# Spreading the unpacking of 4-bit weights over three stages of a transformer block

## The chip, the cores and the metric

The kernel runs on one core of one Trainium2 chip. The metric is the device time of one execution in microseconds. A core has five engines that run side by side, each through its own instructions strictly in order: TensorE (PE in the profile; its weight loads are PEld), VectorE (DVE), ScalarE (ACT), GpSimd (POOL) and SyncE (SP, which here issues transfers only). Transfers (DMAs) are issued by SP, ACT or POOL and are carried by 16 DMA engines that all of them share.

## The reference

Two batches of 1024 tokens, width 1024, everything in 32-bit floats. A layer norm feeds two branches, and their product is added to the input:

```
xn = layernorm(x)                         # (2, 1024, 1024)
q, k = rope(xn @ wq), rope(xn @ wk)       # 32 heads of 32, 8 key/value heads
s  = softmax(causal(q k^T / sqrt(32))) v @ wo
w_gu, w_d = sc[g] * (nibble(qw) - (nibble(qz)[g] + 1))    # 4-bit weights, groups of 128 rows
gate, up = split(xn @ w_gu)               # 2 x 2752 columns
h  = silu(gate) * up
out = x + s * silu(h @ w_d)
```

The 4-bit weights come packed, eight to a 32-bit word along the rows.

## The kernel before

The stages run in this order: norm of batch 0; then for each batch the projection (q, k, v), the attention and the output projection (with wo); then the FFN of both batches. The norm of batch 1 is computed inside the output projection of batch 0.

**Unpacking (`unpack`, L234).** The packed weights are turned into 32-bit floats once, in units, and written to memory in the order in which the FFN loads them: 22 units for the gate and up weights (tensors ng), 12 for the down weights (nd). A unit (`unit`, L238) loads the words (qw, L242) and the zeros (zt, L244) on SP's queue; VectorE masks or shifts the words and adds the zeros (nib, L250 to L255), twice, for the even and the odd nibbles; ScalarE turns the bytes into floats (nf, L259), twice; GpSimd issues the stores (L267). It is a generator: it yields after each of these steps, five times in a unit, and whoever drives it calls `next`. All its buffers come from a pool of three. In batch 0 it makes the units 0 to 16 of gate and up, in batch 1 the other five and all of down, both in the output projection.

**Output projection (`project_out`, L872).** The result is made in 16 parts of 256 tokens by 256 columns, 16 matmuls each (ps_wo, L846). The first two parts are interleaved with the end of the attention (`first`), the other 14 follow here, in six PSUM buffers. At the beginning of each part `next(side)` is called three times, which advances the unpacking; after each part but the first, one tile of 128 tokens of the next batch's norm follows (`norm`, L299: load xt, statistics, std on ScalarE, xn on VectorE, eight transposes ps_ln on TensorE, two copies xnT on ScalarE). Even parts are copied out by VectorE and stored on GpSimd's queue, odd ones by ScalarE and stored on its own (`leave`, wo_r L858, sT L859). What the generator has left is called after the loop.

**Projection (`project`, L336).** k, then q, in blocks of 512 tokens by 128 columns, eight matmuls each (ps_qk, L354; three PSUM buffers). VectorE makes two products of a block (rot, L358 and L360), GpSimd two more operations (L361, L362), ScalarE rounds the result (rot_hi, L364), VectorE takes the rest (rot_lo, L366), and SP stores both halves (ks, qs). The finished keys and queries of the first head group are loaded again as stacks (room, L474 and L479), and TensorE multiplies them between the blocks of the later heads, to find each row's maximum (`rows`, `turns`; s, L514 and L520; VectorE reduces, mx L530). Beside that xn is split into two halves (x_hi L404, x_lo L406) and stored for the FFN (xs, L407 and L408). The argument `side` is advanced once after each block; in batch 0 it is a survey of the scales (`look`), in batch 1 it is empty.

**Attention (`attend`, L571).** Its order is written out by hand in steps of 128 keys. The score products for the maxima of later steps are spread over the steps by a planner; `due` forces those that a coming step needs. When a group is complete, `shifts` reduces the maxima on VectorE (mt, L554), and a step later `shift_rows` transposes them on TensorE (m_ps, L565) for use in the products of the step after that.

Outside the attention, a scheduler orders the instructions of each engine when the kernel is built, by what they depend on; `issue_after` puts an instruction behind a given one. The FFN (L1160) takes PSUM banks that the output projection used, and ScalarE and VectorE take turns at rescaling its accumulators (L930, L932).

Of the kernel before, what the change touches and what calls it, by code (L numbers as in the profile page):

```python
# [23 lines left out]
P = 128  # L24
# [12 lines left out]
def block_kernel(  # L37
# [193 lines left out]
        nc.vector.tensor_scalar(flag, ps, 1.0, None, ALU.min)  # L231
        yield

    def unpack(pool, b):  # L234

        def unit(r, qw_src, z_src, dst, w):  # L238
            qw = pool.tile([P, 2 * P], U32, name="qw")
            zt = pool.tile([P, 2 * P, 2], U16, name="zt")  # L240
            for c0, n, src in qw_src:
                nc.sync.dma_start(qw[:r, c0 : c0 + n], src)  # L242
            for c0, n, src in z_src:
                nc.sync.dma_start(zt[:r, c0 : c0 + n, :], src)  # L244
            nf = pool.tile([P, 4, 2, 2 * P], F32R, name="nf")
            nib = pool.tile([P, 2, 4 * P], U16, name="nib")
            halves = qw.bitcast(U16)
            for i in range(2):
                if i == 0:
                    nc.vector.tensor_scalar(nib[:r, i, : 2 * w], halves[:r, : 2 * w], 0x0F0F, None, ALU.bitwise_and)  # L250
                else:
                    nc.vector.tensor_scalar(
                        nib[:r, i, : 2 * w], halves[:r, : 2 * w], 4, 0x0F0F, ALU.logical_shift_right, ALU.bitwise_and
                    )
                nc.vector.tensor_tensor(  # L255
                    nib[:r, i, : 2 * w], nib[:r, i, : 2 * w], zt.rearrange("p n i -> p (n i)")[:r, : 2 * w], ALU.add
                )
                yield
                nc.scalar.activation(  # L259
                    nf[:r, :, i, :w],  # L260
                    nib[:r, i, :].bitcast(U8).rearrange("p (n b) -> p b n", b=4)[:, :, :w],
                    AF.Copy,
                    bias=-16.0,
                )
                yield
            for c0, n, to in dst:
                nc.gpsimd.dma_start(to, nf[:r].rearrange("p b i n -> p (b i) n")[:, :, c0 : c0 + n].bitcast(F32))  # L267
            yield
# [8 lines left out]
        for f in range(17) if b == 0 else range(17, NF):  # L277
            n = P if f < NF - 1 else FTAIL
            at = [(u * n, n, slice(u * INTER + f * P, u * INTER + f * P + n)) for u in range(2)]
            yield from unit(  # L280
                P,
                [(c0, n, qw_gu[:, cols]) for c0, n, cols in at],
                [(c0, n, zb_gu[:, cols]) for c0, n, cols in at],
                [(u * n, n, to) for u, to in enumerate(ng_rows(f, n))],
                2 * n,
            )
        for r0 in range(0, RD, P) if b == 1 else ():
            r1 = min(RD, r0 + P)
            for c0 in range(0, D, 2 * P):
                cols = slice(c0, c0 + 2 * P)  # L290
                yield from unit(
                    r1 - r0,
                    [(0, 2 * P, qw_d[r0:r1, cols])],
                    [(0, 2 * P, zb_d[r0:r1, cols])],
                    [(0, 2 * P, nd_dram.rearrange("(r s) n -> r s n", s=8)[r0:r1, :, cols])],
                    2 * P,
                )

    def norm(b, xnT, pool, psp, bufs):  # L299

        for t in range(NT):
            xt = pool.tile([P, D], F32, name="xt", bufs=bufs)
            nc.sync.dma_start(xt, x[b, t * P : (t + 1) * P, :])
            stats = pool.tile([P, 2, 6], F32, name="stats")
            for h in range(2):
                nc.vector.bn_stats(stats[:, h, :], xt[:, h * 512 : (h + 1) * 512])
            mv = pool.tile([P, 2], F32, name="mv")
            nc.vector.bn_aggr(mv, stats.rearrange("p h s -> p (h s)"))
            std = pool.tile([P, 1], F32, name="std")
# [4 lines left out]
            nc.vector.tensor_scalar(xn, xt, mv[:, 0:1], rstd, ALU.subtract, ALU.mult)  # L314
            for h in range(NS // 4):
                ps = psp.tile([P, 4, P], F32, name="ps_ln")
                for j in range(4):
                    nc.tensor.transpose(ps[:, j, :], xn[:, (4 * h + j) * P : (4 * h + j + 1) * P], ident)
                nc.scalar.copy(xnT[:, 4 * h : 4 * h + 4, t * P : (t + 1) * P], ps)
            yield  # L320

    def load_w(pool, w_dram, c, **kw):
        return load_w_at(pool, w_dram, c, **kw)[0]
# [12 lines left out]
    def project(b, xnT, w_k, qs, ks, v, side, head):  # L336


        with tc.tile_pool(name="qkv_w", bufs=3, reuse_waits="tile") as wp, tc.tile_pool(name="qkv", bufs=3, reuse_waits="tile") as pool, tc.tile_pool(
# [9 lines left out]
            def turned(w, dst, work=iter(()), blocks=range(NB)):  # L349
                for n in blocks:  # L350
                    tok = slice(n * TB, (n + 1) * TB)
                    ps = psp.tile([P, TB], F32, name="ps_qk")
                    for s in range(NS):
                        nc.tensor.matmul(ps, w[:, s, :], xnT[:, s, tok], start=(s == 0), stop=(s == NS - 1))  # L354
# [216 lines left out]
    def attend(head, v, oT, output):  # L571
# [5 lines left out]
        with ExitStack() as st:  # L577
# [165 lines left out]

# [16 lines left out]
            for i, (g, qb, kt) in enumerate(steps):  # L760
# [111 lines left out]
    def project_out(output, side, turns, xnT, xp):  # L872

        with ExitStack() as st:
# [4 lines left out]
            if xnT is not None:  # L879
                ln = st.enter_context(tc.tile_pool(name="ln", bufs=3, reuse_waits="tile"))  # L880
                ln_ps = st.enter_context(tc.tile_pool(name="ln_ps", bufs=2, space=PSUM, reuse_waits="tile"))
                following = norm(output.b + 1, xnT, ln, ln_ps, 3)
                w_k = load_kv(xp, wk)
            for i, part in enumerate(output.parts):
# [10 lines left out]
            for _ in following:  # L895
                pass
            return w_k

    def load_gu(ring, f, u):
# [509 lines left out]
    for b in range(B):  # L1409
# [5 lines left out]
        with tc.tile_pool(name="at_first", bufs=1, reuse_waits="tile") as fp, tc.tile_pool(  # L1415
# [5 lines left out]
            with tc.tile_pool(name="ps_s", bufs=1, space=PSUM, reuse_waits="tile") as ps_s:  # L1421
# [83 lines left out]
```

## Time and profile before

| what | us |
|---|---|
| median of three runs | 2325.3 (2325.21 to 2326.38) |
| profiled execution | 2326.46 |
| its span, first to last instruction | 2324.7 |
| TensorE busy | 2244.4 (97%) |
| VectorE / ScalarE / GpSimd busy | 1423.5 / 1132.7 / 799.1 |

The stages by their first matmul in the trace: projection of batch 0 at 26.6, its attention at 214, the rest of its output projection at 550.8; projection of batch 1 at 689.4, attention at 869, output projection at 1205.4; the FFN at 1304.2. "Busy" counts from an instruction's start to its end. Idle time is put down to what ended it, "<-" and the engine, operation and line. A wait on TensorE costs time; one on another engine costs only if TensorE comes to wait for it.

### The profile page before, as it was taken

To read this page: it belongs to the slowest core of one execution; us is meant where nothing else is said; L and a number is where in the kernel's file an instruction comes from. 1 tells how busy PE (TensorE), PEld (TensorE's weight loads), DVE (VectorE), ACT (ScalarE), POOL (GpSimd) and SP (SyncE) were. 2 spreads that over 40 slices of the span, in tenths; PEclk is the share of its full clock that TensorE was granted. 3 is DMA by queue.
4 is the path that set the end of the run, shared out by engine and by line. 5 is a ranking of instruction groups with operands and counts; after the bars stand their busy time and mean duration, and the time that the engine had idled before them with its cause. 6 is when DMAs were issued, how large, how long until landed. Compare 5 with 4: busy or idle time off the path is not lost.

```text
span 2324.7 us, 30824 instructions
## 1 busy us (share of the span) xinstructions
PE 2244.4 (97%) x11313; PEld 1549.1 (67%) x11313; DVE 1423.5 (61%) x2270; ACT 1132.7 (49%) x1819; POOL 799.1 (34%) x569
## 2 busy tenths in 40 slices
PE   7999999999699999999999899999999999999987
PEld 4456555557574465555558778888877888888765
DVE  6473777763422526777722367667877777767775
ACT  3013545453430015445533465555787655557775
POOL 1332677773313216777742100000235100001352
PEclk9999999999899999999999899999999999999999
DMA  6664131315974251231229632231746645323465
GB/s 197 215 226 120 46 92 46 80 31 172 298 268 154 91 142 49 49 89 37 73 80 324 213 82 60 77 82 55 281 148 216 179 137 139 101 59 114 153 202 149
DMA packets 262183, 309.50 MB, mean 133 GB/s; under 512 B 19147, under 2 KB 197707, under 8 KB 261880
## 3 DMA queue, kind: packets, MB, share of 16 engines
q1 hardware_dynamic: 245172, 260.62, 37.3%
q0 software_dynamic: 10752, 38.02, 5.1%
q10 hardware_dynamic: 6100, 8.82, 1.2%
q8 instruction: 91, 1.49, 0.3%
q14 instruction: 68, 0.56, 0.1%
HBM read 214.58 MB, written 97.03 MB: 134 GB/s over the span
## 4 chain that ended last, share of the span: by engine, by line
PE 68%; issue 11%; POOL 8%; DMA 5%; DVE 5%; ACT 2%; SPq 1%; POOLq 0%; ACTq 0%; DVEq 0%
PE acc L1160 27%; PE acc L1043 11%; PE s L520 6%; PE st L627 5%; PE o L674 5%; PE ps_wo L846 3%; PE l L692 3%; PE ps_v L374 2%; PE st L642 2%; POOL rot L361 2%; POOL rot L362 2%; PE ps_qk L354 2%; DMA qw<-in_L_ffn_qweight_gu 2%; POOL p L787 1%; DVE mx L530 1%
## 5 line engine op out<-in xcount | busy, mean ns | idle before, releaser
L1160 PE MATMUL acc<-x,w 128*128 128x512 f32 x2752 | 644.3, 395 | 9.2 <-ACT wo_r L858 6.2
L1160 PEld LDWEIGHTS acc<-x,w 128*128 128x128 f32 x2752 | 515.5, 189 | 129.6 <-DVE h L1133 7.5
L530 DVE TENSOR_REDUCE mx<-s 128x1 f32<-128x512 f32 (+3 forms) x672 | 384.2, 607 | 215.0 <-PE s L520 117.4
L932 DVE TENSOR_SCALAR acc<-acc,r_gu 128x1024 f32<-128x1024 f32 x301 | 389.0, 1293 | 178.2 <-PE acc L1160 177.6
L652 ACT ACTIVATE p<-st 128x512 f32<-128x512 f32 (+3 forms) x768 | 314.9, 496 | 312.1 <-PE st L642 312.0
L930 ACT ACTIVATE acc<-acc,r_gu 128x1024 f32<-128x1024 f32 x301 | 327.4, 1088 | 236.3 <-PE acc L1160 227.9
L1144 POOL TENSOR_TENSOR h_lo<-h,h_hi 128x512 fp32r<-128x512 f32 x78 | 100.4, 1289 | 803.6 <-PE acc L1043 588.7
L787 POOL TENSOR_TENSOR p<-p 128x2048 f32<-128x2048 f32 (+3 forms) x122 | 360.7, 2961 | 8.7 <-PE o L674 4.3
L932 DVE TENSOR_SCALAR acc<-acc,r_d 128x512 f32<-128x512 f32 x320 | 241.6, 758 | 67.7 <-PE acc L1043 65.0
L930 ACT ACTIVATE acc<-acc,r_d 128x512 f32<-128x512 f32 x320 | 210.9, 662 | 65.9 <-PE acc L1043 59.1
L354 PE MATMUL ps_qk<-xnT,w_qk 128*128 128x512 f32 x512 | 238.9, 604 | 0.0
L846 PE MATMUL ps_wo<-oT,w_o 128*128 128x256 f32 x1024 | 236.4, 387 | 0.0
L1043 PE MATMUL acc<-h_lo,w 128*128 128x512 f32 (+1 forms) x576 | 228.9, 397 | 2.9 <-POOL h_lo L1144 2.8
L1043 PE MATMUL acc<-h_hi,w 128*128 128x512 f32 (+1 forms) x576 | 229.5, 398 | 0.7 <-ACT h_hi L1143 0.7
L846 PEld LDWEIGHTS ps_wo<-oT,w_o 128*128 128x128 f32 x1024 | 194.5, 193 | 42.1 <-issue 16.7
L674 PE MATMUL o<-p,v 128*32 128x512 f32 (+3 forms) x1536 | 162.2, 494 | 0.8 <-POOL p L655 0.8
L354 PEld LDWEIGHTS ps_qk<-xnT,w_qk 128*128 128x128 f32 x512 | 94.3, 192 | 92.8 <-issue 90.5
L655 POOL TENSOR_SCALAR_AFFINE_SELECT p<-p 128x512 f32<-128x512 f32 x128 | 81.2, 641 | 165.7 <-ACT p L652 161.6
L364 ACT CAST rot_hi<-rot 128x512 fp32r<-128x512 f32 x40 | 24.6, 618 | 229.7 <-POOL rot L362 219.5
L361 POOL TENSOR_TENSOR rot<-rot,cs 128x512 f32<-128x512 f32 x40 | 53.4, 1335 | 236.8 <-DVE rot L360 207.3
L520 PE MATMUL s<-kst,room 128*128 128x512 f32 (+3 forms) x384 | 130.9, 385 | 0.3
L1043 PEld LDWEIGHTS acc<-h_lo,w 128*128 128x128 f32 (+1 forms) x576 | 108.4, 188 | 30.7 <-POOL h_lo L1144 5.2
(163 smaller groups left out, 2478.9 us busy)
## 6 DMA issues: line engine op xcount, KB each, us to landing
w<-ng SPq DMA_DIRECT2D x86, 512.0 KB, 6.0
w<-nd SPq DMA_DIRECT2D x63, 512.0 KB, 3.6
ng<-nf POOLq DMA_DIRECT2D x42, 512.0 KB, 9.1
room<-qs SPq DMA_DIRECT2D x160, 128.0 KB, 3.7
x<-xs SPq DMA_DIRECT2D x32, 512.0 KB, 5.4
qst<-qs SPq DMA_DIRECT2D x96, 128.0 KB, 3.6
xt<-in_L_attn_x SPq DMA_DIRECT2D x16, 512.0 KB, 4.6
w_qk<-in_L_attn_wq SPq DMA_DIRECT2D x16, 512.0 KB, 7.3
```

Of the source, the lines that this page charges most:

```text
L354: nc.tensor.matmul(ps, w[:, s, :], xnT[:, s, tok], start=(s == 0), stop=(s == NS - 1))
L520: nc.tensor.matmul(s[:, c * w : (c + 1) * w], q[j][:, qt * P : (qt + 1) * P], k[:, k0:k1], start=n == 1, stop=c == n - 1 and (n > 1 or not ...
L530: nc.vector.tensor_reduce(mx[:, at, js[0] : js[0] + n, k0 // TB], s[:, : w * n].rearrange("p (j t) -> p j t", j=n), AX.X, ALU.max)
L627: nc.tensor.matmul(s[:, q0:], kst[g][:, kt * P : (kt + 1) * P], stack[g][j][:, qlo + q0 : qlo + TB], start=True, stop=False,)
L652: nc.scalar.activation(p[:, j, q0:], st[j][:, q0:], AF.Exp, scale=1.0 / math.sqrt(HD))
L674: nc.tensor.matmul(o[HD * j : HD * (j + 1), q0:], v[:, kt, HD * g : HD * (g + 1)], p[:, j, q0:], start=(kt == 0), stop=last,)
L787: what(*args)
L846: self.last = nc.tensor.matmul(ps[:, c * self.BLK : (c + 1) * self.BLK], self.ws[c0 + c][:, g, :], self.oT[:, g, t0 : t0 + self.BLK], star ...
L930: nc.scalar.mul(a, a, r)
L932: nc.vector.tensor_scalar(a, a, r, None, ALU.mult)
L1043: nc.tensor.matmul(acc[c], w[:k, c * P : (c + 1) * P], ht[:k, :], start=(f == 0 and t == 0), stop=(t == 1), skip_group_check=(f > 0),)
L1160: nc.tensor.matmul(a[:, n, :], w[i][:, g * P : (g + 1) * P], xs[t][:, g, n * TB : (n + 1) * TB], start=(g == 0 and t == 0), stop=(t == 1), ...
```

## The change

The unpacking is split into three parts: units 0 to 7 of gate and up in the first output projection, units 8 to 19 in the projection of batch 1 (a new pool there, with two buffers for nf), and units 20 and 21 with all of down in the second output projection.

- `unit` becomes `load`, `integers` and `store`, and a list of units is walked: the words and zeros of the next unit are asked for before this unit's integers are made, and a unit's stores are issued within the following unit, at its second step. qw, zt and nib have two buffers. A unit has four yields.
- In the first output projection the unpacking is advanced only from the eighth part on, and its instructions are put behind the norm's last xn (VectorE) and last copy (ScalarE). The norm begins after the first part instead of the second.
- In the projection of batch 1 the unpacking is advanced three times after each block.
- In the attention the rows of maxima are transposed two steps after the maxima instead of one, and the score products are due one step earlier.

```diff
-    def unpack(pool, b):
+    def unpack(pool, gu, down):
...
+        def load(r, qw_src, z_src, dst, w):
+            qw = pool.tile([P, 2 * P], U32, name="qw", bufs=2)
+            zt = pool.tile([P, 2 * P, 2], U16, name="zt", bufs=2)
...
+        def store(nf, r, qw_src, z_src, dst, w):
+            for c0, n, to in dst:
+                nc.gpsimd.dma_start(to, nf[:r].rearrange("p b i n -> p (b i) n")[:, :, c0 : c0 + n].bitcast(F32))
...
+        todo = list(units())
+        came, left = [load(*todo[0])], None
+        yield
+        for i, u in enumerate(todo):
+            if i + 1 < len(todo):
+                came.append(load(*todo[i + 1]))
+            for t, nf in enumerate(integers(*came.pop(0), u[0], u[4])):
+                if t == 1 and left:
+                    store(*left)
+                yield
+            left = nf, *u
+        yield
+        store(*left)
+        yield
...
-            yield
+            yield reads, last
...
-                    next(side, None)
+                    for _ in range(3 if b else 1):
+                        next(side, None)
...
-                        at(now + 1, lambda g=g, h=h, mt=mt: box.update({(g, h): head.shift_rows(mt)}))
+                        at(now + 2, lambda g=g, h=h, mt=mt: box.update({(g, h): head.shift_rows(mt)}))
...
-                if i + 2 < len(steps):
-                    turn(rate * (cost - LATE), 3, steps[i + 2][:2])
+                if i + 3 < len(steps):
+                    turn(rate * (cost - LATE), 3, steps[i + 3][:2])
...
-                    if g == 0:
-                        for _ in range(turns):
-                            next(side, None)
+                    if g == 0 and (xnT is None or i >= NT - 1):
+
+                        with ExitStack() as order:
+                            for last in normed or ():
+                                order.enter_context(tc.issue_after(last.ins))
+                            for _ in range(turns):
+                                next(side, None)
...
-                    if i:
-                        next(following, None)
+                    normed = next(following, normed)
...
-                    project(b, xnT, w_k, qs_dram[b], ks_dram[b], v, iter(()), head)
+                    with tc.tile_pool(name="unpack", bufs=2, side="right", reuse_waits="tile") as up:
+                        side = unpack(up, range(8, 20), False)
+                        project(b, xnT, w_k, qs_dram[b], ks_dram[b], v, side, head)
+                        for _ in side:
+                            pass
...
-            side = unpack(up, b)
+            side = unpack(up, range(8) if b == 0 else range(20, NF), b == B - 1)
```

`integers` is the middle of the old `unit` (both masks, both sums, both conversions), unchanged but for its name and two buffers for nib; `units` lists the same sources and targets as before.

More of the change, by code (lines that the diff above doesn't have):

```diff
@@ L232, in look @@
         yield
-    def unpack(pool, b):
-        def unit(r, qw_src, z_src, dst, w):
-            qw = pool.tile([P, 2 * P], U32, name="qw")
-            zt = pool.tile([P, 2 * P, 2], U16, name="zt")
+    def unpack(pool, gu, down):
+        def load(r, qw_src, z_src, dst, w):
+            qw = pool.tile([P, 2 * P], U32, name="qw", bufs=2)
+            zt = pool.tile([P, 2 * P, 2], U16, name="zt", bufs=2)
             for c0, n, src in qw_src:
@@ L244, in unit, with integers @@
                 nc.sync.dma_start(zt[:r, c0 : c0 + n, :], src)
+            return qw, zt
+        def store(nf, r, qw_src, z_src, dst, w):
+            for c0, n, to in dst:
+                nc.gpsimd.dma_start(to, nf[:r].rearrange("p b i n -> p (b i) n")[:, :, c0 : c0 + n].bitcast(F32))
+        def integers(qw, zt, r, w):
             nf = pool.tile([P, 4, 2, 2 * P], F32R, name="nf")
-            nib = pool.tile([P, 2, 4 * P], U16, name="nib")
+            nib = pool.tile([P, 2, 4 * P], U16, name="nib", bufs=2)
             halves = qw.bitcast(U16)
@@ L257, in unit @@
                 )
-                yield
+                yield nf
                 nc.scalar.activation(
@@ L264, in unit @@
                 )
[L265 to L268, printed above, removed]
+                yield nf
         def ng_rows(f, n):
@@ L275, in ng_rows @@
             return [rows[:, :, u * n : (u + 1) * n] for u in range(2)]
[L277 to L296, printed above, removed]
-                )
+        def units():
+            for f in gu:
+                n = P if f < NF - 1 else FTAIL
+                at = [(u * n, n, slice(u * INTER + f * P, u * INTER + f * P + n)) for u in range(2)]
+                yield (
+                    P,
+                    [(c0, n, qw_gu[:, cols]) for c0, n, cols in at],
+                    [(c0, n, zb_gu[:, cols]) for c0, n, cols in at],
+                    [(u * n, n, to) for u, to in enumerate(ng_rows(f, n))],
+                    2 * n,
+                )
+            for r0 in range(0, RD if down else 0, P):
+                r1 = min(RD, r0 + P)
+                for c0 in range(0, D, 2 * P):
+                    cols = slice(c0, c0 + 2 * P)
+                    yield (
+                        r1 - r0,
+                        [(0, 2 * P, qw_d[r0:r1, cols])],
+                        [(0, 2 * P, zb_d[r0:r1, cols])],
+                        [(0, 2 * P, nd_dram.rearrange("(r s) n -> r s n", s=8)[r0:r1, :, cols])],
+                        2 * P,
+                    )
@@ L313, in norm @@
             xn = pool.tile([P, D], F32, name="xn")
-            nc.vector.tensor_scalar(xn, xt, mv[:, 0:1], rstd, ALU.subtract, ALU.mult)
+            reads = nc.vector.tensor_scalar(xn, xt, mv[:, 0:1], rstd, ALU.subtract, ALU.mult)
             for h in range(NS // 4):
@@ L318, in norm @@
                     nc.tensor.transpose(ps[:, j, :], xn[:, (4 * h + j) * P : (4 * h + j + 1) * P], ident)
-                nc.scalar.copy(xnT[:, 4 * h : 4 * h + 4, t * P : (t + 1) * P], ps)
-            yield
+                last = nc.scalar.copy(xnT[:, 4 * h : 4 * h + 4, t * P : (t + 1) * P], ps)
+            yield reads, last
     def load_w(pool, w_dram, c, **kw):
@@ L883, in project_out @@
                 w_k = load_kv(xp, wk)
+            normed = None
             for i, part in enumerate(output.parts):
@@ L886, in project_out @@
                 for g in output.products(part, ps):
-                    if g == 0:
-                        for _ in range(turns):
-                            next(side, None)
+                    if g == 0 and (xnT is None or i >= NT - 1):
[4 more added lines that the diff above has]
+                                next(side, None)
                 with tc.issue_after(output.last.ins):
-                    if i:
-                        next(following, None)
+                    normed = next(following, normed)
                 output.leave(part, ps, res.tile([P, TB], F32, name="wo_r"))
-            for _ in following:
-                pass
             return w_k
```

## The prediction

> **What bounds the kernel.** I read the busy shares first: TensorE is busy 2244.4 of 2324.7 us, so only its 80 us of idle time, and the half-speed time that follows it, can be won by reordering. Then the list of what TensorE waits for, and the timeline around the longest entries. Two places carry it. The first is the first output projection, in which the norm of batch 1 runs between the parts. Columns: start, length, engine, line, operation, and in brackets the idle time before it.
>
> ```profile
> 566.85 1.04 PE L318 MATMUL ps_ln<-ident,xn 128*128 128x128 f32 x8
> 567.73 7.07 PE L846 MATMUL ps_wo<-oT,w_o 128*128 128x256 f32 x32
> ...
> 591.23 1.97 PE L318 MATMUL ps_ln<-ident,xn 128*128 128x128 f32 x8 [8.65 <-ACT xnT L319]
> 592.99 8.86 PE L846 MATMUL ps_wo<-oT,w_o 128*128 128x256 f32 x32
> ...
> 618.53 1.97 PE L318 MATMUL ps_ln<-ident,xn 128*128 128x128 f32 x8 [7.83 <-ACT xnT L319]
> ...
> 644.56 1.97 PE L318 MATMUL ps_ln<-ident,xn 128*128 128x128 f32 x8 [7.21 <-ACT xnT L319]
> ```
>
> Three waits of 7 to 9 us; after each the same work is slower (1.97 against 1.04, 8.86 against 7.07). The named copy was not the cause: the xn behind it stood on VectorE behind sums of unpacking that waited for zt. The windows say why those loads were late (busy us and counts per engine, then granted clock, DMA share, GB/s; then the same for the second output projection and the FFN's start):
>
> ```profile
> 550.80:689.40 138.60, 113.97 (x527) 98.91 (x524) 55.16 (x135) 58.04 (x82) 36.14 (x42) 0.90 0.94 301
> ```
> ```profile
> 1205.00:1304.00 99.00, 99.00 (x466) 86.99 (x466) 27.92 (x79) 34.05 (x38) 21.63 (x26) 1.00 0.95 323
> 1304.00:1345.00 41.00, 31.76 (x116) 24.25 (x115) 16.25 (x13) 20.05 (x20) 3.78 (x4) 0.83 0.45 121
> ```
>
> The transfers are full in both stages. The second place is the FFN's start:
>
> ```profile
> 1304.16 1.28 PE L1160 MATMUL acc<-x,w 128*128 128x512 f32 x4
> 1311.68 3.78 PE L1160 MATMUL acc<-x,w 128*128 128x512 f32 x8 [6.25 <-ACT wo_r L858]
> 1317.47 22.32 PE L1160 MATMUL acc<-x,w 128*128 128x512 f32 x84 [2.00 <-ACT acc L930]
> ```
> ```profile
> 1309.16 2.00 ACT L259 ACTIVATE nf<-nib 88x1024 fp32r<-88x1024 uint8 x2 [5.35 <-DMA nd<-nf]
> 1311.07 0.56 ACT L858 COPY wo_r<-ps_wo 128x512 f32<-128x512 f32 x1
> ```
>
> ScalarE works in order: the copy that frees TensorE's accumulator stands behind the last unit's conversion, and that waited for a store.
>
> **The change, part by part.** It is a reordering: the built instruction order has the same number of instructions on every engine. All 34 units stay: 17 in each output projection become 8 (first output projection), 12 (second projection) and 14 (second output projection: two of gate/up, twelve of down). A unit loads 2 x 64 KiB of words and 2 x 64 KiB of zeros and stores 2 x 512 KiB: 1.31 MB. VectorE gives it 0.29 + 0.29 + 2 x 0.38 = 1.3 us, ScalarE 2.0, GpSimd 1.7 for issuing two stores.
>
> *The norm first.* The sums of unpacking now stand behind seven of the eight xn on VectorE, its conversions behind the seventh xnT copy. Transfers in that time are small (xt 4.2 MB), so the norm's chain (two stats 1.3, std 0.3, xn 0.8, copies 1.1 us) fits under a part's 7.07. A part with its transposes takes 7.95. Before, 550.78 to 689.37 is 138.6 us; 14 parts at 7.07 plus 8 x 0.88 are 106, and I take 107: TensorE would be through at 658, **31.6 us earlier**. The norm also starts one part earlier; xn was ready at 557.8 and is wanted at 560. No cost.
>
> *What is late next.* The conversions start only after the seventh copy: part 1 ends at 550.8 + 9.2 = 560.0, the seventh transposes at 560.0 + 0.9 + 6 x 7.95 = 608.6, the copies at 610. From there twenty units and some 30 xs stores share the transfers. In the built order, GpSimd's first rotation stands behind the stores of 13 units and its fourth between the two stores of the 19th; ScalarE's fourth rot_hi stands behind all twenty conversions, VectorE's first rotation behind the 15th unit's first sum. SP has the last unit's loads ahead of the third ks stores, and so ahead of the key and query stacks (room). TensorE's first score product needs those stacks. Before, it came at once when TensorE reached it, with 66 projection matmuls in front:
>
> ```profile
> 689.37 27.63 PE L354 MATMUL ps_qk<-xnT,w_kv 128*128 128x512 f32 x64
> 716.84 29.35 PE L354 MATMUL ps_qk<-xnT,w_qk 128*128 128x512 f32 x68
> 745.62 0.79 PE L514 MATMUL s<-mask_q,ident_r 128*128 128x512 f32 x1
> 746.25 0.22 PE L520 MATMUL s<-room,room 128*128 128x128 f32 x1
> ```
>
> Without delay it would now stand at 746.25 - 31.6 = 714.6. The last (20th) conversion waits for the 18th store to land. Bytes from 610 until then: 18 stores 18.9 MB, 17 units' loads 4.5, 29 xs stores 7.6, sT 1.8, three w_qk 1.6, ks 1.5: 35.9 MB. At the window's 301 GB/s that is 119 us, at 323 it is 111: the conversion comes at 721 to 729, I take 724. Then: conversion and rot_hi to 727, rot_lo 728, fifth rotation on VectorE 729.4 and on GpSimd (2 x 1.27) 732, its halves 733.5, sixth rotation 735 and 737.6, then what the trace shows before: from 737.6 to the first stack's load 2.8 us, four loads of 0.46 and 3.2 to landing: **745.3**. That is the 746 of before. The 31 us come back as waits inside the second projection (the fourth block of matmuls already waits for VectorE's first rotation, some 10 us). After the first score nothing differs: TensorE is full to 869. The part's sum: **1 us gained**, between 4 gained and 4 lost by the two bandwidths.
>
> Here a rule is weighed. The Trainium skill, "DMA: Bandwidth & Descriptors", section Bandwidth, holds that transfers between HBM and SBUF are bound at about 358 GB/s for a core, with a fabric ceiling of 435. By 358 the estimate is 100 us, score at 731, 15 us gained; by 435, 82 us and nearly the whole 31. The row decides: 301 GB/s at share 0.94 is the same traffic. The rule against spreading ("Issuing engines are not separate DMA queues": all queues run on the same 16 engines) also speaks against winning by asking early: earlier loads don't make bytes fewer.
>
> *Loads a unit ahead, late stores, nf in two buffers in the projection.* The order of work per unit is unchanged, the queue is full anyway: 0, but see the second rival.
>
> *Second output projection.* Units fall from 17 to 14. Three units less are 3.9 MB, at 323 GB/s 12.2 us: the last conversion moves from 1309.2 to 1297, before TensorE's end at 1304. The copies of parts 9 and 11 go at 1297 to 1298, the last at 1305. So the 6.25 us fall away. Next late: the first rescale of ScalarE, which came 3.6 us after the last sT store was issued (1312.74 to 1316.33); the store is now issued at 1305.7, so about 1309, and TensorE waits from 1306.8 (twelve matmuls after 1304.16) to 1310 instead of resuming at 1317.47: **7.5 us**. Half speed: after 1317.47 the 84 matmuls took 22.3 us where 0.2275 each (two members in 1.82) make 19.1. The skill's "TensorE: Matmul & The Clock Gate", Part 1, halves the clock after an idle window of about 3.4 us; the rows agree at 7 to 9 us (slow) and 0.8 (1.15 for 1.04), and say nothing at 3. By the rule 3.2 us are won; if the new wait throttles as well, none. I take **2.9**; sum **10.4**, between 5 and 11.
>
> *Rows of maxima a step later.* In attention TensorE is full (99.14 of 100 us from 260 to 360). The waits at the rows' transposes:
>
> ```profile
> PE m_ps L565 <- DVE mx L530: 2.7, 12, 0.2
> ```
>
> That is the bank being read, not the maxima being late; the 3.2 us wait for mt lies in the first projection, which the edit does not touch. Score products due a step earlier only change places. 2.7 gained at most, the same lost if banks clash; I take **0.6 gained**.
>
> Sum 1 + 10.4 + 0.6 = 12.0 us. The profiled execution took 2326.46, 1.76 outside the span; its median is 2325.3. 2326.5 - 12.0 = 2314.5, and 1.2 less for the median: **2313.3**.
>
> **Rivals.** *A: the transfers keep up.* For: queues mix kinds, xs stores have long rows, and 650 to 689 moved 312 GB/s at share 0.91. Against: 0.94 with two thirds of the same bytes. At 358 GB/s 15 us instead of 1: 2299; with no delay 2283. *B: slower.* In the projection nf has two buffers. A buffer's turn is 2.1 conversion + 1.8 issue + 9.1 (median landing of ng) = 13.0 us, so 6.5 per unit; eight units at 5.45 (555.8 to 643.0 in 16 steps) reach 654, seven xs pairs 16 more, twelve units 78: the last conversion at 748, first score at 769, 23 us late, less the 11 won elsewhere: 2337. It decides from 6 us per unit on (conversion after 741). Against: two thirds of the landing was queueing. *C: ScalarE at the FFN's start is held by something else* (the store's landing, the branch), and nothing is won there: 2324. *D: the norm still waits*, because loads of two units run ahead of it: same bound at 746, so no other time than the forecast.
>
> **Numbers.** Forecast 0.53 (own range 2306 to 2321), A 0.20, B 0.15, C 0.12. A measurement tells apart 0.2%, 4.7 us. Faster: 0.53 x 0.92 + 0.20 = 0.69; slower: B and a little of C, 0.16; the rest 0.15. Range 2296 to 2332 leaves out the ends of A and B.
>
> **What would show it.** Right: no waits at ps_ln, output projection done at 658; then idle TensorE before ps_qk matmuls waiting for VectorE's rotations, and the first score within 742 to 750; DMA share above 0.9 from 610 to 720; FFN resumed by 1310 relative to its start at 1304. Wrong: a first score at 715 to 735 (A) or past 755 (B); a wait of 6 us at wo_r still there (C).

## The result, and the profile after

The changed kernel takes 2329.17 us (median of 9 runs, 2327.7 to 2330.16) against 2324.99 before (9 runs, 2320.95 to 2327.58): **slower**, by 4.2 us or 0.18% in the medians; the ratio over all runs is 1.0025, 95% interval 1.0016 to 1.0034. Forecast were 2313.3 and faster. The span of the profiled execution grew from 2324.7 to 2327.4 us. By stages, each from its first matmul to that of the next (us):

| stage | before | after | change |
|---|---|---|---|
| to the first product of attention 0 | 214.2 | 214.6 | +0.4 |
| attention 0, to the rest of its output projection | 336.6 | 338.2 | +1.6 |
| from there to the first score product of batch 1 | 195.5 | 204.9 | **+9.4** |
| from there to attention 1 | 122.7 | 124.3 | +1.6 |
| attention 1 | 336.4 | 338.0 | +1.6 |
| second output projection | 98.8 | 98.8 | 0 |
| FFN start, to its 97th matmul | 36.5 | 24.2 | **-12.3** |
| the rest | 984.1 | 984.5 | +0.4 |

The FFN gained its 12 us; the stretch before the first score product, the stage behind it and both attentions lost 14.2. First TensorE's timeline after, in the same columns as before:

```profile
561.94 1.04 PE L341 MATMUL ps_ln<-ident,xn 128*128 128x128 f32 x8
562.81 7.07 PE L870 MATMUL ps_wo<-oT,w_o 128*128 128x256 f32 x32
...
617.29 41.60 PE L870 MATMUL ps_wo<-oT,w_o 128*128 128x256 f32 x192
658.73 7.03 PE L377 MATMUL ps_qk<-xnT,w_kv 128*128 128x512 f32 x16
667.24 14.00 PE L377 MATMUL ps_qk<-xnT,w_kv 128*128 128x512 f32 x32 [1.49 <-ACT wo_r L882]
703.27 10.21 PE L377 MATMUL ps_qk<-xnT,w_kv 128*128 128x512 f32 x16 [22.02 <-DVE rot L383]
...
722.17 7.13 PE L377 MATMUL ps_qk<-xnT,w_qk 128*128 128x512 f32 x16 [1.82 <-DVE rot L383]
736.37 17.61 PE L377 MATMUL ps_qk<-xnT,w_qk 128*128 128x512 f32 x36 [7.07 <-DVE rot L383]
...
757.64 0.44 PE L544 MATMUL s<-room,room 128*128 128x128 f32 x1 [3.44 <-DMA room<-qs]
```

The transposes of the norm no longer wait, and the output projection is done at 658.7. Then TensorE stands: 22 us before the fourth block of the projection (its PSUM buffer is freed by VectorE's first rotation), 9 more at later blocks, and 3.4 us until the first key and query stacks (room) have landed. The windows tell why (busy us and counts per engine; then granted clock, DMA share, GB/s):

```profile
552.80:610.00 57.20, 57.20 (x297) 50.76 (x294) 25.59 (x57) 13.26 (x28) 2.48 (x4) 1.00 0.50 161
610.00:625.00 15.00, 15.00 (x75) 13.27 (x74) 4.10 (x13) 10.51 (x14) 4.84 (x6) 1.00 0.85 239
610.00:735.00 125.00, 93.97 (x327) 61.86 (x325) 42.36 (x103) 51.88 (x64) 43.36 (x50) 0.90 0.94 290
655.00:685.00 30.00, 24.76 (x67) 12.11 (x65) 10.00 (x23) 10.30 (x14) 4.18 (x5) 1.00 0.81 249
```

For 57 us, while the norm has VectorE and ScalarE for itself, the transfers run half empty. For the 125 us after that they are nearly full, except from 610 to 625, where the unpacking starts, and from 655 to 685: from 634.5 to 667.3 SP issues no load of the unpacking, since nine pairs of xs stores stand in front. What those 125 us cost VectorE stands in its list of waits from 640 to 760 (total, times, longest):

```profile
DVE x_lo L430 <- DMA xs<-x_lo: 25.0, 10, 7.7
DVE rot_lo L389 <- ACT rot_hi L387: 14.2, 4, 4.1
DVE nib L258 <- DMA qw<-in_L_ffn_qweight_gu: 12.9, 5, 4.2
DVE nib L263 <- DMA zt<-zb_gu: 12.6, 8, 3.7
```

Its first rotation stands behind x_lo's that wait for an earlier xs store to land, and behind sums that wait for their words and zeros. The FFN's start, by contrast, is clean:

```profile
1318.70 3.11 PE L1186 MATMUL acc<-x,w 128*128 128x512 f32 x12
1322.51 19.54 PE L1186 MATMUL acc<-x,w 128*128 128x512 f32 x84 [0.69 <-ACT acc L956]
```
```profile
1305.73 2.00 ACT L267 ACTIVATE nf<-nib 88x1024 fp32r<-88x1024 uint8 x2 [4.24 <-DVE nib L263]
1307.64 0.56 ACT L882 COPY wo_r<-ps_wo 128x512 f32<-128x512 f32 x1
```

The last conversion ends 11 us before TensorE reaches the FFN; no wait for wo_r is left, and the 84 matmuls take 19.5 us instead of 22.3. Last, the attention, in TensorE's list of waits for attention 0 alone (st: the score products of the step itself; p: their exp; l and o: the row sums and values made from p):

```profile
PE st L651 <- ACT p L676: 3.0, 8, 0.4
PE l L716 <- POOL p L811: 0.6, 1, 0.6
```

No wait is left at the rows' transposes, but eight waits of 0.4 us for the softmax's weights p; over both attentions they are 16 (6.0 us), where before had 4 (1.5 us).

### The profile page after: what moved, and what is told of

Same layout as the page of the kernel before. It is cut to its first block, busy times and chain, and to the rows that moved or that the text cites. A ratio compares the mean times of both kernels' runs of the same rounds, so it can differ in the third digit from the quotient of the medians.

```text
span 2327.4 us, 30813 instructions
## 1 busy us (share of the span) xinstructions
PE 2244.1 (96%) x11313; PEld 1537.6 (66%) x11313; DVE 1428.3 (61%) x2270; ACT 1133.9 (49%) x1819; POOL 796.6 (34%) x569
## 4 chain that ended last, share of the span: by engine, by line
PE 74%; issue 9%; POOL 7%; DMA 5%; ACT 2%; DVE 2%; SPq 1%; ACTq 0%; POOLq 0%; DVEq 0%
PE acc L1186 27%; PE acc L1069 11%; PE ps_wo L870 8%; PE st L651 7%; PE s L544 6%; PE o L698 5%; PE l L716 3%; PE st L666 2%; POOL rot L384 2%; POOL rot L385 2%; DMA xs<-x_hi 1%; PE s L538 1%; POOL p L811 1%; PE ps_v L398 1%; DMA zt<-zb_gu 1%
## 5 line engine op out<-in xcount | busy, mean ns | idle before, releaser
L1069 PEld LDWEIGHTS acc<-h_hi,w 128*128 128x128 f32 (+1 forms) x576 | 108.4, 188 | 30.6 <-issue 2.9
```

Source lines behind the costliest of these rows:

```text
L1069: nc.tensor.matmul(acc[c], w[:k, c * P : (c + 1) * P], ht[:k, :], start=(f == 0 and t == 0), stop=(t == 1), skip_group_check=(f > 0),)
```

## The experiments

All kernels were timed beside the kernel before; ratios are to it. The first stage differs by up to 5 us between profiled executions (210.9 to 215.8) though nothing touches it, so stages are compared rather than spans. "The long stage" is the one from the rest of the first output projection to the first score product of batch 1: 195.5 us before, 204.9 after.

**The rows of maxima undone.**

```diff
-                        at(now + 2, lambda g=g, ...
+                        at(now + 1, lambda g=g, ...
-                if i + 3 < len(steps): turn(..., steps[i + 3][:2])
+                if i + 2 < len(steps): turn(..., steps[i + 2][:2])
```

> The kernel after, with the edit of the rows of maxima alone undone (shift rows a step after the maxima, score products due two steps ahead). Theory: the edit costs 1.6 us in each attention (336.57 to 338.20 and 336.39 to 337.95 between the traces), so both attentions go back to 336.4 to 336.6 us and the time falls by 3.2 us, to 2326.0 (2325.0 to 2327.0). Rival: the attentions are longer for another reason (where the tiles lie, what is left over from the projection before them): both stay at 338 and the time at 2329.2.

Measured: 2326.41 us, ratio 1.0004 (0.9996 to 1.0012); attentions 336.5 and 336.4. Its waits in attention 0:

```profile
PE m_ps L589 <- DVE mx L554: 1.4, 6, 0.2
PE l L716 <- POOL p L811: 0.8, 1, 0.8
PE st L651 <- ACT p L676: 0.6, 2, 0.4
```

The edit does remove the six waits of 0.2 us, and brings six of 0.4 at st instead. In the trace, near 271.4, the undone kernel has a score product s between the values o and the next st; with products due a step earlier that place is empty, and st waits for ScalarE's exp that frees its bank. The edit costs 1.6 us per attention, **3.2 us** in all. All of TensorE's listed waits in attention 0 come to 4.0 us against 3.2, so they make up 0.8 of it at most; TensorE's busy time is 1.3 us longer (334.0 against 332.7), and what lengthens it was not traced.

**Three buffers in the second projection.**

```diff
-                    with tc.tile_pool(name="unpack", bufs=2, ...
+                    with tc.tile_pool(name="unpack", bufs=3, ...
```

> The kernel after, with three buffers in place of two for the converted integers and the words in the second projection. Theory (bytes through full transfers set the last conversion): nothing moves, the last conversion stays within 3 us of 734.2, the first score product of batch 1 within 3 us of 757.6, time 2329 (2327 to 2331). Rival (turn-around of two buffers sets it): the last conversion comes 8 us or more earlier, and the time is 2320 or less.

The edit gives a third buffer to the converted integers (nf) alone: words, zeros and nib have their two written out at the tile, and keep them. Measured: 2334.17 us, ratio 1.0044 (1.0032 to 1.0056). The last unit's conversions began 177.7 us after the stage's start instead of 181.4, yet the long stage grew to 212.5.

```profile
761.71 0.45 PE L544 MATMUL s<-room,room 128*128 128x128 f32 x1 [13.53 <-DMA room<-qs]
```

And SP's waits between 690 and 765:

```profile
SPq L498 <- DMA ks<-rot_hi: 6.8, 1, 6.8
...
SPq L391 <- DMA w_kv<-in_L_attn_wv: 5.3, 1, 5.3
SPq L503 <- DMA qs<-rot_hi: 4.7, 1, 4.7
```

The two buffers were not what cost the time: a third moved the conversion by 3.7 us, less than half of what the rival asked for, and the score product came later. But the theory failed too: "nothing moves" was wrong. SP, which issues in order, waits for the small stores of keys and queries to land before it loads the stacks, and these landings took longer (in the kernel after its longest wait for one is 1.0 us). That a third unit's stores stand in front of them is the reading that fits; it was not measured transfer by transfer. Shown is that the last conversion alone does not set the first score product.

**Units from the second part on.**

```diff
-                    if g == 0 and (xnT is None or i >= NT - 1):
+                    if g == 0 and (xnT is None or i >= 1):
```

> The kernel after, but the eight units of the first output projection are asked for from its second part on, not from its eighth, still queued behind each part's norm on VectorE and ScalarE. Theory (the half-empty transfers while the norm runs, 161 GB/s at share 0.50 for 57 us, are what was lost): about 8 MB move into that stretch, the first score product comes 28 us earlier, near 730, and the time is 2301 (2293 to 2312), if the norm does not wait again. Rival (the norm waits again behind the unpacking's sums, as before the change): idle time at the transposes of the norm of 15 us and more, and a time of 2320 or more.

Measured: 2313.63 us, ratio 0.9953 (0.9941 to 0.9966); long stage 190.3.

```profile
552.80:610.00 57.20, 57.20 (x299) 50.30 (x298) 32.92 (x81) 27.48 (x43) 16.06 (x19) 1.00 0.95 304
```

The stretch is now full: (304 - 161) GB/s x 57.2 us = 8.2 MB more, as expected, and the norm does not wait. But 14.5 us came of it, not 28, and the time is above its expected range. TensorE still stood 17.7 us before its fourth block, and VectorE shows for what:

```profile
695.00 0.69 DVE L430 TENSOR_TENSOR x_lo<-xnT,x_hi 128x512 fp32r<-128x512 f32 x1 [5.95 <-DMA xs<-x_lo]
...
701.48 0.69 DVE L430 TENSOR_TENSOR x_lo<-xnT,x_hi 128x512 fp32r<-128x512 f32 x1 [4.24 <-ACT wo_r L882]
...
703.39 0.68 DVE L381 TENSOR_TENSOR rot<-ps_qk,cs 128x512 f32<-128x512 f32 x1
```

The last conversion was over at 690; all sixteen x_lo stand before the first rotation, two buffers deep, and waited for stores in full transfers (317 GB/s at share 0.98 from 690 to 704).

**The pairs of x_hi and x_lo behind their column's rotation**, the units as in the kernel after (`turns` holds the last rotation's instructions on GpSimd, ScalarE and VectorE and its second store on SP):

```diff
                 for n in range(NB):
                     tok = slice(n * TB, (n + 1) * TB)
+                    with ExitStack() as order:
+                        for last in turns if b else ():
+                            order.enter_context(tc.issue_after(last.ins))
-                    hi = xp.tile(...)
+                        hi = xp.tile(...)
...
```

> The kernel after, with the sixteen pairs of x_hi and x_lo (8.4 MB of stores) each queued behind the last rotation of their column; the units stay where the kernel after has them. Theory (what counts is the bytes that go through full transfers before the first stacks, whichever they are): some 6 to 8 MB leave that stretch, at 290 GB/s 21 to 28 us, the stage to the first score product falls from 205 to 178 to 186, time 2307 (2301 to 2314). Rival (it is the units' own conversions, sums and stores in front of the rotations on ScalarE, VectorE and GpSimd, and the pairs only fill gaps): stage 196 or more, time 2320 or more.

Measured: 2306.55 us, ratio 0.9925 (0.9912 to 0.9939); long stage 179.4. No unit was moved, and the last conversion came 23.7 us earlier in the stage (157.8 instead of 181.4). The waits before the blocks fell from 31 us to 7; the next stage is 127.3, 2.9 longer. The wait for the stacks is now the largest:

```profile
728.51 0.44 PE L548 MATMUL s<-room,room 128*128 128x128 f32 x1 [8.03 <-DMA room<-qs]
```

The time is as the bytes would have it, but the run does not tell bytes from order. With the pairs, the x_lo's in front of VectorE's first rotation and the xs stores in front of SP's loads went too: the first load of the second projection's units is issued at 646.9, after 13.4 us of waiting for a store of the first units to land, instead of at 667.3.

**The twelve units behind the rotations of their blocks** (`turns` as above, for each block).

```diff
-                    for _ in range(3 if b else 1):
-                        next(side, None)
+                    with ExitStack() as order:
+                        for last in turns if b else ():
+                            order.enter_context(tc.issue_after(last.ins))
+                        for _ in range(3 if b else 1):
+                            next(side, None)
```

> The kernel after, with the twelve units of the second projection each queued behind the rotation of the block that they are asked for after, on VectorE, ScalarE, GpSimd and SP, so that they run through the later projection, whose transfers are nearly idle (share 0.24 to 0.32 from 750 to 841 before). Theory (twenty units in front of the first rotations are what holds the first score product): the rotations no longer wait, the first score product comes at 716 to 728, and the time is 2295 (2287 to 2303). Rival (bytes of the region decide, wherever they stand, or the unpacking now delays the maxima of the score products by as much): the stage from the first score product to attention 1 grows from 124.3 by 25 us or more, time 2320 or more.

Measured: 2303.7 us, ratio 0.9917 (0.9904 to 0.993); long stage 176.7, the next 126.5.

```profile
666.17 20.87 PE L377 MATMUL ps_qk<-xnT,w_kv 128*128 128x512 f32 x48 [0.61 <-ACT wo_r L885]
688.35 27.73 PE L377 MATMUL ps_qk<-xnT,w_qk 128*128 128x512 f32 x64 [1.32 <-DVE rot L383]
...
729.24 0.44 PE L547 MATMUL s<-room,room 128*128 128x128 f32 x1 [8.21 <-DMA room<-qs]
```

The 31 us of waits for rotations are 3.3; what is left is the stacks' landing. The first score product (729.2) and the time both lie just beyond the slow end of their expected ranges (728 and 2303); the theory's mechanism is there, and the rival's growth of 25 us is 2.2.

**The order inside a unit put back** (loads at its own turn, stores at once):

```diff
-        for i, u in enumerate(todo):
-            if i + 1 < len(todo): came.append(load(*todo[i + 1]))
...
+        for u in units():
+            for nf in integers(*load(*u), u[0], u[4]):
+                yield
+            store(nf, *u)
+            yield
```

> The kernel after, with the order inside a unit put back: a unit's words and zeros are loaded at its own turn and its stores are begun right after its last conversion. Theory (bytes through full transfers, and small transfers queued behind them): nothing of note changes, the stage from the rest of the first output projection to the first score product stays at 205 us within 4, the FFN's start keeps its gain of 12, time 2329 (2325 to 2333). Rival 1 (asking ahead and storing late is what makes the queues longer): that stage falls to 198 or less, time 2322 or less. Rival 2 (the gain at the FFN's start comes from loads ahead and late stores, not from three units fewer): the FFN's first wait for wo_r comes back and the time is 2336 or more.

Measured: 2331.26 us, ratio 1.0032 (1.0021 to 1.0044), not told apart from the kernel after; long stage 204.1, FFN start as in the kernel after. In the kernel after, this part of the change is worth nothing that could be measured.

**The kernel before with 20 and 14 units** instead of 17 and 17:

```diff
-        for f in range(17) if b == 0 else range(17, NF):
+        for f in range(20) if b == 0 else range(20, NF):
```

> The kernel before, with twenty units in the first output projection and fourteen in the second (17 and 17 before); the norm, the order inside a unit and the rows of maxima as before. It has the unit counts of the kernel after on both sides, without the holding back. Theory (the units before the first score product are the same twenty, and what costs is that they start 57 us later): the FFN's start gains the same 12 us, and the 3.9 MB of three more units delay the first score product by 0 to 13 us; I take 6: stage 195.5 to 202, time 2319 (2313 to 2326). Rival (twenty units alone cost what the kernel after lost, held back or not): stage 205 or more, time 2322 to 2327; if the FFN's start gains nothing here, the gain was not from the count.

Measured: 2319.44 us, ratio 0.9977 (0.9967 to 0.9987); long stage 200.0. The FFN's start, and then TensorE's longest item of waits:

```profile
1309.51 3.11 PE L1160 MATMUL acc<-x,w 128*128 128x512 f32 x12
1313.06 19.56 PE L1160 MATMUL acc<-x,w 128*128 128x512 f32 x84 [0.44 <-ACT acc L930]
```
```profile
PE ps_ln L318 <- ACT xnT L319: 26.0, 5, 8.8
```

Here the FFN's start takes 24.0 us, so the whole gain there comes of three units fewer. The three units cost 4.5 us before the first score product, with the norm waiting 26 us on the way. The kernel after has the same twenty units there and a norm without waits, and is 4.9 us worse: **by these stages the 9.4 us are 4.5 for more units and 4.9 for the rest of the arrangement**.

**Three edits together**: units from the second part on, units behind their blocks' rotations, rows of maxima undone.

> The kernel after with three edits together: units of the first output projection from its second part on, the twelve units of the second projection behind the rotations, the rows of maxima undone. Theory: the eight units are through by 620 instead of 650, so the sixteen pairs of x_hi and x_lo no longer wait in full transfers, the first rotation comes at 670 or before and TensorE passes the second projection nearly without a wait; the stage to the first score product falls from 176.7 (paced alone) to 166 to 172, the attentions to 336.5 each: time 2303.7 - 3.3 - 7 = 2293 (2288 to 2298). Rival (only the pacing counts; the small transfers wait behind the units' stores all the same): 2300 or more.

Measured: **2286.02 us**, ratio 0.9834 (0.9821 to 0.9847), 39 us under the kernel before and better than the range expected. Long stage 163.2, the next 124.6, attentions 336.5 and 336.4.

```profile
657.31 27.63 PE L377 MATMUL ps_qk<-xnT,w_kv 128*128 128x512 f32 x64
684.78 29.35 PE L377 MATMUL ps_qk<-xnT,w_qk 128*128 128x512 f32 x68
...
714.52 0.30 PE L547 MATMUL s<-room,room 128*128 128x128 f32 x1 [0.16 <-DMA room<-qs]
```

TensorE passes from the output projection to the scores without a wait worth naming. The 31.6 us of the prediction are there, once nothing stands in the way.

**The same, and the pairs spread as well.**

> As the run with three edits together, and the pairs of x_hi and x_lo of each column also queued behind that column's last rotation, in the order they are traced. Theory: the first rotation then has nothing in front of it, TensorE passes the first 66 matmul groups of the second projection without a wait but for what the first stacks' loads cost, stage 164 to 168, time 2290 (2286 to 2295). Rival (the pairs and units now stand between the later rotations and the maxima and delay them): the stage from the first score product to attention 1 grows by 3 us or more over 124.3 and the time is 2295 or more.

Measured: 2288.75 us, ratio 0.9844 (0.9831 to 0.9857). Long stage 164.5, as expected; but the next stage grew to 128.6, with four waits of TensorE (4.1 us) for the maxima. The rival's mechanism is there, in small. The intervals of this kernel and the last overlap, so spreading the pairs as well is not shown to cost or to win.

In its profile attention 1 takes 337.9 us, 1.5 more, though the rows are undone: TensorE's granted clock is halved there for 3.4 us from 1150.4 on, at a wait of 0.8 us that the kernel with the three edits has too, at full clock. Two of the kernels below show the same (338.1 with the order inside a unit put back, 337.9 with 11 and 9 units).

**The three edits, with the order inside a unit put back.**

> As the run with three edits together (units early, paced, rows of maxima undone), and the order inside a unit put back to the kernel before: loads at the unit's own turn, stores at once. Theory (loads a unit ahead keep a unit's sum from holding the next xn on VectorE when units run beside the norm in full transfers): waits before the norm's transposes come back, 5 to 15 us in all, time 2294 (2289 to 2302). Rival (queueing each unit behind the norm's instructions is enough): no such waits, 2284 to 2288.

Measured: 2307.53 us, ratio 0.9923 (0.991 to 0.9937). Right in direction, but above its range and wrong in place: the norm does not wait. The stage after the first score product takes 141.1 us instead of 124.6. TensorE's waits from 714 to 860, and one of VectorE's:

```profile
PE s L538 <- DVE mx L548: 6.7, 4, 3.2
PE ps_v L392 <- ACT v L395: 3.2, 1, 3.2
PE s L538 <- DMA room<-qs: 2.9, 1, 2.9
```
```profile
DVE nib L258 <- DMA qw<-in_L_ffn_qweight_gu: 14.9, 6, 6.1
```

A unit pinned behind a rotation asks for its words there, and VectorE waits for them in front of the maxima. With three edits together that wait does not occur. So the order inside a unit (loads ahead and stores late), worth nothing in the kernel after, is worth some 20 us in the better arrangement (2307.5 against 2286.0). The waits for words point to the loads; the late stores were not put back alone.

**The three edits, without queueing the units behind the norm.**

> As the run with three edits together, without queueing the units of the first output projection behind the norm's instructions; loads still a unit ahead. Theory: the sums may stand ahead of an xn again, but their loads were asked for a unit earlier, so the waits before the norm's transposes are shorter than the 24 us of before: 3 to 12 us, time 2292 (2287 to 2299). Rival (loads ahead alone keep the norm free): 2284 to 2288.

Measured: 2295.36 us, ratio 0.9872 (0.9857 to 0.9887). One wait is back, and the transposes after it take 1.97 us instead of 1.04:

```profile
591.45 1.97 PE L341 MATMUL ps_ln<-ident,xn 128*128 128x128 f32 x8 [7.67 <-DVE rstd L335]
```

Long stage 174.3, 11 us more. Queueing behind the norm is worth 9 us here; the loads ahead do not replace it.

**The three edits with 11 and 9 units** and four steps of unpacking a part.

> As the run with three edits together, with eleven units in the first output projection (four steps of unpacking a part in place of three) and nine in the second projection. Theory: the transfers moved only 109 GB/s from 640 to 670 there, so three more units (3.9 MB, 13 us) fit before the second projection's stores, and the later projection has three units fewer beside its score products, whose waits of 2.5 us shrink: 2285 (2282 to 2288). Rival (the first output projection is full, the units run into the pairs of x_hi and x_lo and the first rotation waits again): stage to the first score product 170 or more, 2291 or more.

Measured: 2293.1 us, ratio 0.9867 (0.9852 to 0.9883); a miss. Two waits (5.3 us) for copies of xnT came back. In ScalarE's order the first of these copies stands behind a std that waited 5.8 us for VectorE's statistics, the second behind a conversion that waited 3.6 us for its sum. Neither theory had named that; long stage 168.8, 5.6 more, and attention 1 has the 1.5 us at half clock.

## Why the prediction was wrong

The forecast was a gain of 12.0 us on the span; measured is a loss of 2.7 between the two profiles. Step by step:

- **The norm first**: right. No waits at the transposes, output projection through in 106 us (forecast 107), at 658.7. The transfers in the norm's time were 9.2 MB (57.2 us x 161 GB/s) where 4.2 were named, at no cost to it.
- **What is late next**: the mechanism was right, its size was not, and this is the step that failed. Forecast: "the conversion comes at 721 to 729, I take 724", first score product at 745.3, "1 us gained". Measured: last conversion at 734.2, score product at 757.6. Counted from the stage's start, the conversion is 8.2 us later than forecast and the rest of the chain took 23.4 us instead of 21.3. The bytes were right (125 us x 290 GB/s = 36.2 MB; forecast 35.9). The mis-sized term is the rate: 114 us for 35.9 MB are 315 GB/s, chosen between two windows of before (301 and 323) and taken for the whole stretch; measured are 290. From 610 to 625 it was 239, and from 655 to 685, where the loads stood behind the xs stores in SP's queue, 249. In the other 80 us the remaining 25.2 MB make some 315, as forecast. The pace of full transfers was right; that they would always have work was not. The prediction's own sign, a share above 0.9 from 610 to 720, was met on average (0.93), which hid both stretches. With the half-speed matmuls after the last wait (1.6 us) the part lost 11.0 us instead of gaining 1.
- What the step did not see at all: it took the order as given. Putting the sixteen pairs with their 8.4 MB of stores behind the rotations gave 25 us of the long stage, pacing the units 28, filling the half-empty 57 us 14.5. And the chain behind the last conversion is made of small transfers whose landing is itself at stake, as three buffers showed.
- **Loads a unit ahead, late stores, nf in two buffers: 0**: right for this kernel, measured by putting each back.
- **Second output projection and FFN start**: 10.4 forecast, within 5 to 11; measured 12.3, and the case with 14 units alone shows that it is the count. The wait that remains was forecast at some 3 us and is 0.7; half speed gave 2.8 (forecast 2.9).
- **Rows of maxima**: forecast 0.6 gained, at most 2.7 lost; measured 3.2 lost. The 2.7 us at m_ps did vanish. "Score products due a step earlier only change places" was the error: near 271.4 a product had covered the exp, and at st there are now 16 waits of up to 0.4 us instead of 4.
- The rivals: the slow one (two buffers for nf) named the right place, and its sign, a first score past 755, was met (757.6), but not its cause: the last conversion came at 734.2, before its "after 741", and with three buffers for nf the time was worse. Transfers that keep up, at the 358 GB/s of the Trainium skill ("DMA: Bandwidth & Descriptors", section Bandwidth), were rightly set back behind the row of 301; the measured 290 lies lower still. The other two did not come about: no wait for wo_r is left at the FFN's start, and the norm does not wait.

The sum: forecast +12.0; the stretch -12.0 against forecast, the rows -3.8, the FFN +1.9, unexplained -0.8 (0.4 of it before attention 0): -2.7.

## What to carry to other kernels

When transfers are full on both sides of a move, work held back has to be paid later, and the queues that it is moved into decide what it delays: look for a stretch where the transfers are really idle (in the kernel before, from 750 to 841, share 0.24 to 0.32) before deciding what to hold back. A rate read from a full stretch holds only while the queues that feed it have work to issue. Order background work behind the foreground's instructions on each engine that it uses, the issuing one too, and ask for its data one unit ahead, or its first wait stands in front of the work it was meant to fill. A wait that a reordering leaves uncovered can be longer than the one it removes, so ask of each moved instruction what it was hiding.

## What the runs showed of the hardware

SP can take longer to issue when the transfers are full. In the kernel after, the same two loads of zeros took 0.84 us of SP at 673 and 3.09 at 691; the windows beside them (columns as above) have the transfers at shares 0.49 and 1.00:

```profile
673.81 0.84 SPq L244 DMA_DIRECT2D zt<-zb_gu  x2
...
691.15 3.09 SPq L244 DMA_DIRECT2D zt<-zb_gu  x2
```

```profile
670.00:677.00 7.00, 7.00 (x18) 3.15 (x17) 4.08 (x13) 3.75 (x4) 1.45 (x2) 1.00 0.49 122
688.00:701.00 13.00, 0.00 (x0) 0.00 (x0) 3.23 (x8) 5.14 (x6) 3.72 (x6) 0.50 1.00 310
```

Full transfers can thus slow not only the landing but the queue that asks. They do not always: at 705.7, between 700 and 715 at share 1.01, the same two loads took 0.91 us. What else has to come together stays open.

The half-speed time after a wait shows again outside the norm: in the kernel after, a wait of 3.4 us before the first score product is followed by four projection matmuls in 3.33 us (first fence); without the wait, in the kernel with units from the second part on, in 1.93 (second).

```profile
757.89 3.33 PE L377 MATMUL ps_qk<-xnT,w_qk 128*128 128x512 f32 x4
```
```profile
743.88 1.93 PE L377 MATMUL ps_qk<-xnT,w_qk 128*128 128x512 f32 x4
```

The rule that the prediction weighed for the FFN's start (the Trainium skill, "TensorE: Matmul & The Clock Gate", Part 1: an idle window of about 3.4 us halves the clock) agrees with this wait, and with the granted clock, which is halved for 3.4 us from 757.3 on. But half clock also came at a shorter wait: at the end of attention 1, in the kernel with the pairs spread as well, 0.8 us of waiting were followed by eight matmuls (l) in 1.94 us at half clock; with the three edits alone the same wait was followed by the same matmuls in 1.07. So the length of one wait does not decide it here.
